# The place of the scaling of energy tile 7 in ScalarE's queue, in a cross-attention kernel on one core

## The chip, the cores and the metric

The kernel runs on one core of a Trainium2 chip. The metric is the time of one execution in microseconds (us) on the device. Engines are named as in the profile: PE is TensorE's matmuls and PEld its weight loads, DVE is VectorE, ACT is ScalarE, POOL is GpSimd, SP issues most of the DMAs.

## The reference

For each of 32 batches there are `x` and `y` of 256 channels by 1024 positions. Cut to what matters:

```
x_q = einsum('oc,bcn->bno', w_qk, y)
x_k = einsum('oc,bcn->bon', w_qk, x)
x_v = einsum('oc,bcn->bon', w_v, x) + b_v
energy = einsum('bnc,bcm->bnm', x_q, x_k)          # 1024 x 1024 for each batch
attention = softmax(energy, axis=-1)
attention = attention / (1e-07 + attention.sum(axis=1, keepdims=True))
x_r = einsum('bcn,bnm->bcm', x_v, attention)
x_r = relu(einsum('oc,bcn->bon', w_t, x - x_r) + b_t)
out = x + x_r
```

The softmax goes along rows of the energy matrix; the second division goes by sums over its columns, so all rows of a batch must be done before the attention is complete.

## The kernel before

**Energies.** Since `w_qk` serves queries and keys alike, the kernel forms g = (w_qk^T w_qk) x once per batch, and a row of energies is y^T g. Both operands are split into parts that TensorE multiplies in one pass: `yf` and `gf` hold, for 2 blocks of 128 channels, three forms each (index 0, 1, 2). A tile of energies (class `Energy`, line 420) is 128 rows by 1024 columns and fills a pair of PSUM banks. `NT` is 8, so a batch has tiles 0 to 7; tile n uses pair n mod 4 of the eight banks (in the last batch, 31, pair n mod 3).

A tile goes through five steps:

- `first()`: 8 matmuls of 128 by 512 (forms 0 and 1, two channel blocks, two halves of the columns; the first half's four come first).
- `scaled()`: ACT multiplies the pair in place by the constant `-OVER`. For tiles 0 to 6 this is one instruction over 1024 columns. For tile 7 it is two, of 512 columns, one for each bank.
- `second()`: 4 matmuls (form 2), added on top of the scaled values, two for each half. Then a DVE reduce over the 1024 columns takes the minimum into `nm`, a column of 128 numbers.
- `exp()`: ACT reads the pair and writes `e`, row block n, with `nm` as bias, and a second ACT instruction reads out the row sums `rs`.
- `share()`: DVE takes the reciprocal `ri` of `rs` and adds `e * ri` to `acc`, the column sums of the batch.

**The order.** The wrappers `pe`, `dve`, `act`, `pool` (class `InOrder`, line 62) keep each engine's instructions in the order in which the program writes them. So the code is the schedule: an instruction that waits holds back all that is written behind it for the same engine. Engines wait for one another by semaphores that follow from the tiles' reads and writes.

The loop over n (line 712) writes the work of a batch as `first(n)`, `exp(n-2)`, `scaled(n)`, `second(n-1)`, `share(n-2)`. On PE this gives `first(7)`, `second(6)`, and behind the loop `second(7)`. On ACT it gives `exp(4)`, `scaled(6)`, `exp(5)`, `scaled(7)` (two instructions), and behind the loop `exp(6)`, two copies out of PSUM, `exp(7)`. On DVE it gives the reduce of tile 5, `share(4)`, the reduce of tile 6, and behind the loop the reduce of tile 7, `share(5)`, `share(6)`, `share(7)`.

**Behind the loop** (line 740 on), for all batches but the last: seven products of half size for the next batch's g (class `Keys`; its products `p1` to `p7` use banks 0, 1 and 2, and `kept` copies a bank to SBUF on ACT: `p1s`, `p5s`, `w`), interleaved with seven for the next batch's values (class `Values`, banks 3, 4 and 5). DVE meanwhile does the three shares, sums `acc` into column totals (`columns`, `inverse`) and gets their reciprocals `rc`. Then `Attention.run` (line 557): DVE's `normal` multiplies `e` by `ri` and `rc` in pieces of 128 by 512, and `mix` forms sums of its quadrants in `et` (`t1`, `t2`, `t3`, `t4`); PE's `epart` multiplies `e` and `et` into three PSUM banks. The quadrant sum `t1` comes in two pieces (`mix(self.t1, ..., j)`, j = 0 and 1), and the product `epart(self.two, 5)`, 8 matmul instructions, reads the first piece with its first four and the second with its last four. The eviction and the stores follow, and the next batch's energies.

Of the kernel before, what the change touches and what calls it, by code (L numbers as in the profile page):

```python
# [17 lines left out]
def kernel(  # L18
# [26 lines left out]
    NT = N // P  # L45
# [41 lines left out]
    def load(b, pieces=1):  # L87
        to = xp.tile([P, KC, N], F32, tag="x", name=f"x_{b}")
        from_ = x[b].rearrange("(k p) n -> p k n", p=P)
        W = KC // pieces  # L90
        for j in range(pieces):
            nc.sync.dma_start(to[:, ts(j, W)], from_[:, ts(j, W)])
        loaded[b] = to
# [115 lines left out]
    def temp(tag, name):  # L209
        return cp.tile([P, MB], F32, tag=tag, name=name)  # L210
# [8 lines left out]
    def summed(b):  # L219

        s = up.tile([P, 4, MB], F32, tag="xs", name=f"xs_{b}")
        t1, t3, t4, t2 = (s[:, j] for j in range(4))
        to = loaded[b]
        b11, b12 = to[:, 0, ts(0, MB)], to[:, 0, ts(1, MB)]
        b21, b22 = to[:, 1, ts(0, MB)], to[:, 1, ts(1, MB)]
        if b == 0:
            pool.tensor_tensor(t1, b11, b12, ALU.add)
            pool.tensor_tensor(t2, b22, t1, ALU.add)
            pool.tensor_tensor(t3, b12, b22, ALU.add)
            pool.tensor_tensor(t4, b21, t2, ALU.add)  # L230
            steps = []
        else:
            q = quarters(x[b])
            nc.sync.dma_start(s[:, :2], q[:, 0, 1:2, :].to_broadcast([P, 2, MB]))
            nc.sync.dma_start(s[:, 2:], q[:, 1])
            steps = [
                lambda: accumulate(s[:, :2], corners(x[b])),
                lambda: accumulate(s[:, 2:], s[:, 0:1].to_broadcast([P, 2, MB])),
                lambda: accumulate(t4, q[:, 1, 1]),
            ]  # L240
        return (b11, b21, b22, t4, t1, t2, t3), steps
# [389 lines left out]
    def columns(b):  # L631

        dve.tensor_reduce(
            parts[:, :, 0],
            acc.rearrange("p (j r) -> p j r", r=G32),
            AX.X,
            ALU.add,
            apply_transpose=True,
        )
# [5 lines left out]
    def inverse(b):  # L645


        sc = one.tile([P, NB, 1], F32, tag="sc", name=f"sc_{b}")
        s = sc[:, :, 0]
        for a in range(1, NG):  # L650
            moved(parts[:G32, :, a], parts[ts(a, G32), :, 0])
        dve.tensor_reduce(s[:G32], parts[:G32], AX.X, ALU.add)
        dve.reciprocal(s[:G32], s[:G32])
        moved(s[G32 : 2 * G32], s[:G32])
        moved(s[2 * G32 :], s[: 2 * G32])
        rc = one.tile([P, NB, G32], F32, tag="rc", name=f"rc_{b}")
        dve.transpose(rc.rearrange("p j r -> p (j r)"), sc.to_broadcast([P, NB, G32]))
        return rc.rearrange("p j r -> p (j r)")
# [49 lines left out]
    for b in range(B):  # L708
        more = b + 1 < B
        rows = []  # L710

        for n in range(NT):
            now = Energy(b, n, q.to, g.split.to)
            rows.append(now)
            now.first()
            if n > 1:
                rows[n - 2].exp()
            now.scaled()
            if n == 1:
                e = ep.tile([P, NT, N], F32, tag="e", name=f"e_{b}")  # L720
                acc = one.tile([P, N], F32, tag="acc", name=f"acc_{b}")
            if n > 0:
                rows[n - 1].second()
            if b == 0 and n == 1:
                u.p4()
                u.c21()
                xsteps[1]()
                xsteps[2]()
                ur, usteps = u.factors()
                for step in usteps:  # L730
                    step()
            if more and b > 0 and n == 0:
                load(b + 1)
                xn, xsteps = summed(b + 1)
            if 1 < n < NT - 1:
                rows[n - 2].share()
            if more and b > 0 and n in (2, 4, 6):
                xsteps[n // 2 - 1]()

        if more:  # L740
            q = Queries(b + 1)
            for i in range(KC):
                q.load(i, nc.sync.dma_start)
            g = Keys(b + 1, xn)
            rows[-1].second()
            rows[-2].exp()
            rows[-3].share()
            g.p1()
            g.p5()
            rows[-1].exp()  # L750
            rows[-2].share()
            rows[-1].share()
            g.p2()
            g.p6()
            columns(b)
            g.p3()
            un = Values(b + 1, xn)
            un.p1()
            g.p7()
            g.c11()  # L760
            g.c12()
            un.p5()
            un.p2()
            un.p6()
            g.c22()
        else:
            rows[-1].second()
            rows[-2].exp()
            rows[-3].share()
            before.xpart(before.one, 7, True)  # L770
            rows[-1].exp()
            rows[-2].share()
            before.epart(before.one, 7)
            ur, usteps = u.factors()
            now = Attention(b, xr, ur)
            now.begin()
            rows[-1].share()
            columns(b)
            for step in usteps:
                step()  # L780
            before.p7s = temp("w", "p7s")
            act.copy(before.p7s, before.one)
        rc = inverse(b)
        if more:
            q.parts(0)
            q.lower(0)
            un.p3()
            g.p4()
            g.c21()
            un.p7()  # L790
            q.parts(1)
            q.lower(1)
            q.mixed(0)
            g.split.parts(0)
            q.mixed(1)
            g.split.lower(0)

            def between():
                g.split.parts(1)
                g.split.lower(1)  # L800
                g.split.mixed(0)
                g.split.mixed(1)

            now = Attention(b, xr, ur)
            now.begin()
            now.run(un, between=between)
            pool.tensor_copy(behind, now.t4[:, HT - 1, :1])
            if b + 2 < B:
                now.close()
                ur, usteps = un.factors()  # L810
                for step in usteps:
                    step()
            else:
                now.epart(now.two, 3, (3,))
                now.c12()
                now.put()
            before = now
            xr, u = xn, un
        else:
            before.end()  # L820
            now.run(None, before)
            now.finish()
# [30 lines left out]
```

## Time and profile before

| | |
|---|---|
| time of 3 runs | 2110.22, 2110.35, 2110.40 us (median 2110.35) |
| time of the profiled execution | 2109.47 us |
| its span in the trace | 2107.7 us |
| granted TensorE clock | 1.0 |
| busy | PE 2083.9 us (99%), DVE 1778.4 (84%), ACT 1150.8 (55%), POOL 674.3 (32%) |
| reduce into `nm`, 256 of them | 1.225 us each |
| exponential, 256 of them | 1.12 us each |

A busy PE is not a PE at its peak: the profile models the ends of matmuls, and a wait shorter than such an end does not show as idle time. Nearly all instructions carry line 73, that of the wrapper, so groups are told apart by what they write and read: `banks<-gf,yf` are energies, `nm<-banks` the reduces, `e<-banks,nm` the exponentials, `banks<-banks` on ACT the scalings. An execution repeats the same pattern once per batch, 65.13 us apart.

### The profile page before, as it was taken

How to read it: one execution, taken by the hardware profiler on the slowest of the kernel's cores; microseconds unless marked ns; L12 is line 12 of the kernel's file. 1: busy time of each engine (PE TensorE's matmuls, PEld its weight loads, DVE VectorE, ACT ScalarE, POOL GpSimd, SP SyncE). 2: the span in 40 equal slices, each digit the busy share in tenths (PEclk: the TensorE clock that was granted, in tenths of full speed). 3: DMA queues.
4: the chain of work that ended last, by engine and by line, in shares of the span. 5: the costliest groups of instructions: out<-in, count | busy, mean ns of one | idle time of the engine just before them, and what ended most of it. 6: DMA issues, size and time to landing. Idle time of an engine off the chain costs nothing.

```text
span 2107.7 us, 21688 instructions
## 1 busy us (share of the span) xinstructions
PE 2083.9 (99%) x7586; PEld 1283.9 (61%) x7586; DVE 1778.4 (84%) x2264; ACT 1150.8 (55%) x1570; POOL 674.3 (32%) x574
## 2 busy tenths in 40 slices
PE   8999999999999999999999999999999999999999
PEld 6556656566665666656665556655566665666664
DVE  6898888988888988889888898888988888988898
ACT  5456554565455664556645556554565455664562
POOL 3322333323333133332333322333323333133321
PEclk9999999999999999999999999999999999999999
DMA  4756577665776656766558766577665776656740
GB/s 140 169 121 145 130 175 170 129 148 128 165 174 148 132 133 152 180 156 132 137 136 184 168 123 142 132 176 169 127 146 129 169 170 146 137 130 157 180 95 30
DMA packets 107788, 306.03 MB, mean 145 GB/s; under 512 B 10656, under 2 KB 11424, under 8 KB 107680
## 3 DMA queue, kind: packets, MB, share of 16 engines
q0 software_dynamic: 57040, 170.68, 44.2%
q1 hardware_dynamic: 50496, 133.85, 18.7%
q8 instruction: 60, 0.98, 0.2%
q14 instruction: 48, 0.39, 0.1%
q10 hardware_dynamic: 144, 0.13, 0.0%
HBM read 124.78 MB, written 33.55 MB: 75 GB/s over the span
## 4 chain that ended last, share of the span: by engine, by line
PE 91%; DVE 3%; ACT 3%; issue 0%; DVEq 0%
PE banks L73 91%; DVE nm L73 2%; ACT e L73 2%; ACT banks L73 1%; DVE e L73 1%; DVE et L73 0%; DVE acc L73 0%; DVE parts L73 0%; DVE rc L73 0%; DVE sc L73 0%; DVEq L73 0%; DVE z L73 0%; DVE ri L73 0%
## 5 line engine op out<-in xcount | busy, mean ns | idle before, releaser
L73 PE MATMUL banks<-gf,yf 128*128 128x512 f32 x3072 | 726.2, 395 | 13.5 <-ACT banks L73 13.4
L73 PEld LDWEIGHTS banks<-gf,yf 128*128 128x128 f32 x3072 | 571.2, 188 | 162.3 <-ACT banks L73 33.3
L73 DVE TENSOR_REDUCE nm<-banks 128x1 f32<-128x1024 f32 x256 | 313.5, 1225 | 158.3 <-PE banks L73 145.6
L73 ACT ACTIVATE e<-banks,nm 128x1024 f32<-128x1024 f32 x256 | 286.7, 1120 | 154.2 <-DVE nm L73 154.2
L73 PE MATMUL banks<-et,us 128*128 128x512 f32 x768 | 348.8, 596 | 1.0 <-DVE et L73 1.0
L73 DVE SCALAR_TENSOR_TENSOR e<-e,ri,rc 128x512 f32<-128x512 f32 x512 | 347.7, 746 | 1.1
L73 DVE SCALAR_TENSOR_TENSOR acc<-e,ri,acc 128x1024 f32<-128x1024 f32 x224 | 289.3, 1291 | 8.0
L73 ACT ACTIVATE banks<-banks 128x1024 f32<-128x1024 f32 (+1 forms) x288 | 261.2, 915 | 49.0 <-PE banks L73 48.8
L73 PEld LDWEIGHTS banks<-et,us 128*128 128x128 f32 x768 | 143.2, 190 | 191.1 <-issue 161.7
L73 PE MATMUL banks<-e,ut 128*128 128x512 f32 x512 | 225.0, 592 | 0.0
L73 POOL DMA_DIRECT2D yf<-yfr x62 | 53.1, 856 | 528.9 <-ACT yf L73 528.9
L73 ACT ACTIVATE z<-banks,bt 128x512 f32<-128x512 f32 x31 | 21.4, 689 | 340.0 <-DMA out_dram<-z 340.0
L73 PEld LDWEIGHTS banks<-e,ut 128*128 128x128 f32 x512 | 97.2, 190 | 122.7 <-issue 100.2
L73 DVE TENSOR_TENSOR et<-e 128x1024 f32<-128x1024 f32 x128 | 153.7, 1222 | 4.4
L73 POOL TENSOR_TENSOR ut<-ut,bu 128x1024 f32<-128x1024 f32 x64 | 155.5, 2536 | 0.0
L73 POOL DMA_DIRECT2D gf<-gf x62 | 53.1, 856 | 301.5 <-DMA gf<-gfr 257.5
L73 DVE SCALAR_TENSOR_TENSOR z<-z,x 128x512 f32<-128x512 f32 x96 | 136.2, 1419 | 3.3
L73 ACT ACTIVATE yf<-yf 128x1024 fp32r<-128x1024 f32 x124 | 124.3, 1050 | 2.0
L73 PE MATMUL banks<-e,us 128*128 128x512 f32 x256 | 125.3, 592 | 0.0
L73 ACT ACTIVATE gf<-gf 128x1024 fp32r<-128x1024 f32 x124 | 124.2, 1049 | 2.0
L73 POOL DMA_DIRECT2D xs<-xs x31 | 37.2, 1201 | 261.1 <-DMA xs<-in_x_dram 251.6
L73 PEld LDWEIGHTS banks<-wvtTs,xs 128*128 128x128 f32 x768 | 98.2, 192 | 29.6 <-issue 29.6
(104 smaller groups left out, 2614.3 us busy)
## 6 DMA issues: line engine op xcount, KB each, us to landing
yfr<-in_ctx_dram SPq DMA_DIRECT2D x64, 512.0 KB, 5.7
out_dram<-z SPq DMA_DIRECT2D x128, 256.0 KB, 3.4
x<-in_x_dram SPq DMA_DIRECT2D x31, 1024.0 KB, 7.6
xs<-in_x_dram SPq DMA_DIRECT2D x62, 512.0 KB, 5.0
yf<-yfr POOLq DMA_DIRECT2D x62, 512.0 KB, 5.1
yf<-yf POOLq DMA_DIRECT2D x62, 512.0 KB, 7.9
gf<-gfr POOLq DMA_DIRECT2D x62, 512.0 KB, 10.3
gf<-gf POOLq DMA_DIRECT2D x62, 512.0 KB, 5.2
```

The costliest lines, as they stand in the source:

```text
L73: self.last = getattr(self.engine, name)(*args, **kwargs)
```

## The change

In a batch's last turn of the loop (n = 7) the scaling of tile 7 is written ahead of the exponential of tile 5. All other turns keep the exponential in front, and nothing is added or taken away.

```diff
             now.first()
+            order = [now.scaled]
             if n > 1:
-                rows[n - 2].exp()
-            now.scaled()
+                order.insert(int(n + 1 == NT), rows[n - 2].exp)
+            for step in order:
+                step()
             if n == 1:
```

On ACT the order `scaled(6)`, `exp(5)`, `scaled(7)`, `exp(6)` becomes `scaled(6)`, `scaled(7)`, `exp(5)`, `exp(6)`. The queues of the other engines keep their order.

## The prediction

> **What bounds the kernel now.** I read the page first, then the chain of waits, then the timelines of PE, ACT and DVE around one batch's last energy tile. The page:
>
> ```profile
> PE 2083.9 (99%) x7586; PEld 1283.9 (61%) x7586; DVE 1778.4 (84%) x2264; ACT 1150.8 (55%) x1570; POOL 674.3 (32%) x574
> ...
> PE banks L73 91%; DVE nm L73 2%; ACT e L73 2%; ACT banks L73 1%; DVE e L73 1%; DVE et L73 0%; DVE acc L73 0%; DVE parts L73 0%; DVE rc L73 0%; DVE sc L73 0%; DVEq L73 0%; DVE z L73 0%; DVE ri L73 0%
> ```
>
> PE carries 91% of the chain; a reduce, an exponential and a scaling carry nearly all the rest. The chain in order of time shows where:
>
> ```profile
> 1024.52 1.24 DVE nm L73
> 1025.78 1.21 ACT e L73 x2
> 1026.98 0.50 ACT banks L73
> 1027.48 0.04 issue
> 1027.53 62.03 PE banks L73 x224
> ```
>
> So once per batch the chain leaves PE: reduce of tile 5, exponential 5, scaling of tile 7, and then PE again for 62.03 us. The batches are 65.13 us apart, and the same five pieces stand in each. ACT and DVE there (start, duration, engine, operation; in brackets the idle time before and what ended it):
>
> ```profile
> 1025.78 1.12 ACT L73 ACTIVATE e<-banks,nm 128x1024 f32<-128x1024 f32 x1 [0.60 <-DVE nm L73]
> 1026.79 0.19 ACT L73 ACTIVATION_READ_ACCUMULATOR e<-banks,nm 128x1 f32 x1
> 1026.88 1.07 ACT L73 ACTIVATE banks<-banks 128x512 f32<-128x512 f32 x2
> 1028.50 1.11 ACT L73 ACTIVATE e<-banks,nm 128x1024 f32<-128x1024 f32 x1 [0.54 <-DVE nm L73]
> ...
> 1027.24 1.23 DVE L73 TENSOR_REDUCE nm<-banks 128x1 f32<-128x1024 f32 x1
> 1028.85 1.23 DVE L73 TENSOR_REDUCE nm<-banks 128x1 f32<-128x1024 f32 x1 [0.39 <-PE banks L73]
> 1029.99 0.15 DVE L73 RECIPROCAL ri<-rs 128x1 f32<-128x1 f32 x1
> ```
>
> And PE, with one wait of its weight loads 23 us later:
>
> ```profile
> 1025.84 1.29 PE L73 MATMUL banks<-gf,yf 128*128 128x512 f32 x5
> 1027.53 1.22 PE L73 MATMUL banks<-gf,yf 128*128 128x512 f32 x4 [0.39 <-ACT banks L73]
> 1028.58 1.02 PE L73 MATMUL banks<-x,g 128*128 128x512 f32 x2
> ...
> 1051.10 0.30 PEld L73 LDWEIGHTS banks<-et,us 128*128 128x128 f32 x2 [0.66 <-DVE et L73]
> ```
>
> The five matmuls from 1025.84 are the last of `first(7)` and the four of `second(6)`; the four from 1027.53 are `second(7)`. Matmuls of this shape start 0.227 us apart (12 of them to a tile's 2.72), so `second(7)` could have started at 1025.84 + 5 x 0.227 = 1026.97. It starts 0.56 late, and its four take 1.05 instead of 0.91, since its second half waits for the second scaling. PE loses 0.70 us in this place, of which the page's idle column names 0.39.
>
> **The change, part by part.** No instruction is added or removed; three keep their durations and change places on ACT.
>
> *Scaling 7 moved ahead.* Its first half needs the first four matmuls of `first(7)`: the fourth starts at 1025.84 - 4 x 0.227 = 1024.93, ends 0.39 later at 1025.32. ACT comes free of the scaling of tile 6 at about 1025.2 (1024.16 + 1.01). The second half needs the last one, 1025.84 + 0.39 = 1026.23; with 0.04 for the semaphore it runs from 1026.27 to 1026.83 (0.56). Both are done before PE ends `second(6)` and wants the tile at 1026.97. The whole 0.70 of PE's loss goes, if nothing else comes late.
>
> *Exponential 5 behind it.* It is ready at 1025.75 (end of its reduce) and now waits in the queue for the second half. The two halves stand 0.52 apart, start to start, so it starts at about 1026.27 + 0.52 = 1026.79, 1.0 later than now. Queued behind it on ACT is exponential 6, which starts at 1028.50 because its reduce ends at 1028.46. Exponential to next instruction takes 1.10 (1025.78 to 1026.88), so ACT is free at 1027.89: 0.61 to spare, and the delay ends there. Who waits for exponential 5: `share(5)` on DVE, which comes behind two reduces, at 1029.5 at the earliest; and the product that overwrites its bank, `g.p2`, at 1030.30 now and about 1029.6 then. Its sums are out by 1028.0. So this edit costs nothing; without that cover its price is 1.0 us per batch less the 0.61.
>
> *Reduce of tile 7.* It starts at 1028.85 now because `second(7)` ends late. With the 0.70 back, PE has the tile ready near 1028.15. But DVE started the reduce of tile 6 at 1027.24, and that one does not move: its four matmuls lie ahead of the wait. How soon a reduce follows a reduce without a wait no row shows directly. The nearest row is the reciprocal behind the reduce, 1028.85 to 1029.99, 1.14, found so 189 times. The other side is the batch in which the two reduces came closest, 1.26 apart. I take 1.14, since the queue's next instruction reads other data in both cases. So the reduce starts at 1028.38 instead of 1028.85: DVE gains 1.61 - 1.14 = 0.47, not 0.70.
>
> The Trainium skill ("VectorE: DVE Perf Modes", The DRAIN you can't avoid) says that the next operation does not start until the pipe is empty, though one that is not held may start earlier. Taken strictly that makes the spacing a full 1.225, where the row above shows 1.14; the sum below would then be 12.7 us, an estimate, instead of 15.4.
>
> *Which of the two gains counts.* DVE works without a gap from this reduce through shares, column sums, `normal` and the two pieces of `t1` until 1051.04. PE works from 1027.53 without a wait until it needs the second piece of `t1`: the weight load at 1051.10 is released by it. Eight matmuls there take 3.53 (1049.39 to 1052.92) instead of 8 x 0.43 = 3.43, so 0.10 is already lost. DVE is thus level with PE at 1051, and PE, arriving 0.70 earlier, will wait until DVE is done, 0.47 earlier. The batch gains 0.47; PE's wait for `t1` grows from 0.10 to about 0.33 us. Nothing in DVE's chain may lag: exponential 7 starts at 1030.98 now, behind two copies that follow `g.p1` and `g.p5`. Then the copies start at 1029.60 and 1030.08, exponential 7 at 1030.56, its sums come at 1031.77, and `share(7)` wants them at 1032.78 - 0.47 = 1032.31. That leaves 0.54.
>
> *Behind 1051* both engines are shifted by 0.47, and so are the stores, POOL's adds and DMA issues that hang on them. The next energies start on PE 0.47 earlier. Period: 65.13 to about 64.66.
>
> *The sum.* By the distances of the two reduces: 27 batches have 1.61, so 27 x 0.47 = 12.7. The first has 2.20 (gain 1.06), the last 1.41 (0.27; there too DVE's chain sets the end, as PE waits for `e` and `et`), and three have 1.26, 1.79 and 1.76 (0.12, 0.65, 0.62). Together 2.7, in all 15.4 us. The profiled execution of 2109.47 us (span 2107.7) would become 2094.1. The median of the runs lies 0.88 above the profiled one, and 2110.35 - 15.4 = 2095.0.
>
> Bounds: with the reduces 1.26 apart the gain is 0.12 less in each of 32 batches, 15.4 - 3.8 = 11.6, giving 2098.8. With PE's whole loss back it is 27 x 0.70 = 18.9, and for the five others 1.21, 0.70, 1.05, 0.85 and 0.50 by their own gaps: 23.2, giving 2087.2.
>
> **The rivals.**
>
> *DVE does not hold PE* (8%): the whole 0.70 comes back. For it: PE is 91% of the chain, DVE's waits are far smaller. Against: the weight load at 1051.10 waits for DVE. Time about 2087.
>
> *The second scaling is released later than I think* (9%), so that the change does only part of what it says. Now both halves start behind exponential 5, when every matmul they could wait for is done. So the trace does not show whether the second waits for the last matmul of `first(7)` or for the last of `second(6)`. In the latter case it starts at 1026.74 + 0.39 + 0.04 = 1027.17 instead of 1027.40: 0.23 gain for PE and the reduce alike. 27 x 0.23 = 6.2, and some 2 from the others: 2102.
>
> *Slower* (3%): exponential 5 becomes late for what follows. The place is ACT's queue: exponential 5, then 6, two copies, 7, and `share(7)` on DVE. There is 0.61 to spare at exponential 6 and 0.54 at `share(7)`. The delay beyond the 1.0 counted must pass 1.15 before DVE feels it, and 1.15 + 0.47 = 1.62 before the batch is slower than now. If the scaling were held for one tile's turn more (2.72), a batch would lose 2.72 - 1.62 = 1.10, in all 34 us: about 2144. Against it: `first(7)` is finished on PE before all this and waits for nothing that ACT does later.
>
> *No change* (3%): PE loses at another wait what it gains here, the one for `t1` growing by 0.70. This needs DVE's reduce to stay at 1028.85, with PE's end of `second(7)` no longer its reason. Nothing points to it. Time 2110.
>
> **How the numbers follow.** The forecast holds 77%. The range 2089 to 2102 takes in its upper bound 2098.8 and reaches up to the second rival and most of the way down to the first. Differences below 0.2% (4.2 us) can't be told from no change here. Faster by more than that are the forecast and the first two rivals, 94%; within it 3%; slower 3%.
>
> **What would show it.** In the changed profile ACT should have the two scalings of 512 columns ahead of exponential 5, and the exponential starting about 1.0 after the end of its reduce instead of at once. PE's matmuls of `second(7)` should follow `second(6)` 0.227 apart, and the 13.4 us of PE waiting for ACT's `banks` should be gone. The reduces of tiles 6 and 7 should stand 1.14 apart, exponential 6 should still start right behind its reduce, and the weight load for the second piece of `t1` should wait longer by 0.2 to 0.25. The chain should no longer hold the reduce, exponential and scaling of this place; it should pass through DVE's shares, `normal` and `t1` instead. Wrong would be: reduces further apart than 1.3, a wait in `share(5)` or `share(7)` for `rs`, or a batch period not near 64.66.

## The result and the profile after

The changed kernel takes 2096.4 us (median of 6 runs, 2095.36 to 2097.67) against 2110.38 us of the kernel before (6 runs, 2110.22 to 2110.73). The ratio is 0.9934, 95% interval 0.9921 to 0.9946: a small gain, clear of the noise. The forecast was 2095.0, range 2089 to 2102. The profiled execution took 2096.0 us (span 2094.2), 13.5 less than the profiled one before; the forecast had 15.4.

The page of the changed kernel, busy time and the chain of waits by line:

```profile
PE 2080.7 (99%) x7586; PEld 1289.2 (62%) x7586; DVE 1774.5 (85%) x2264; ACT 1145.9 (55%) x1570; POOL 674.7 (32%) x574
...
PE banks L73 72%; DVE e L73 12%; DVE et L73 4%; DVE gfr L73 3%; DVE rc L73 2%; DVE sc L73 2%; DVE parts L73 1%; DVE acc L73 1%; DVE nm L73 0%; DMA gf<-gf 0%; DVEq L73 0%; DVE ri L73 0%; DVE z L73 0%; ACT ow L73 0%
```

Busy shares tell nothing: PE has 99% as before. The chain does: PE falls from 91% to 72%. The reduce, the exponential and the scaling are out of it, and DVE's work between the column sums and `t1` has come in. The timeline of the same batch as in the prediction, 6.49 us earlier by now:

```profile
1018.93 0.58 ACT L73 ACTIVATE banks<-banks 128x512 f32<-128x512 f32 x1 [0.24 <-PE banks L73]
...
1019.77 0.58 ACT L73 ACTIVATE banks<-banks 128x512 f32<-128x512 f32 x1 [0.27 <-PE banks L73]
1020.27 1.11 ACT L73 ACTIVATE e<-banks,nm 128x1024 f32<-128x1024 f32 x1
1020.75 2.35 DVE L73 TENSOR_REDUCE nm<-banks 128x1 f32<-128x1024 f32 x2
...
1022.01 1.11 ACT L73 ACTIVATE e<-banks,nm 128x1024 f32<-128x1024 f32 x1 [0.54 <-DVE nm L73]
```

The two scalings stand ahead of exponential 5, each started by PE. The exponential starts 1.0 after its reduce has ended (1018.03 + 1.22 = 1019.25), and exponential 6 still starts as soon as its own reduce is done. The two reduces are one line now (x2), without a gap: 1.14 apart instead of 1.61. PE in the same place, one run of twelve matmuls without a break (the last four of `first(7)`, then `second(6)` and `second(7)`) and then the next batch's product:

```profile
1018.67 2.88 PE L73 MATMUL banks<-gf,yf 128*128 128x512 f32 x12
1021.39 1.02 PE L73 MATMUL banks<-x,g 128*128 128x512 f32 x2
```

12 x 0.227 = 2.72 is the whole distance, so the 0.70 us are back. Further on, the weight load for the second piece of `t1`, the eight matmuls that read `t1`, and where the chain passes to them:

```profile
1044.14 0.30 PEld L73 LDWEIGHTS banks<-et,us 128*128 128x128 f32 x2 [0.89 <-DVE et L73]
```

```profile
1042.20 3.93 PE L73 MATMUL banks<-et,us 128*128 128x512 f32 x8
```

```profile
1041.50 1.33 DVE e L73 x2
1042.84 0.02 issue
1042.86 1.24 DVE et L73
1044.10 0.04 issue
```

The weight load waits 0.89 instead of 0.66, and the eight matmuls take 3.93 instead of 3.69. Of PE's time 0.33 us are lost here in each batch, where 0.10 were lost before. The period is 64.67 us (65.13 before).

### The profile page after: what moved, and what is told of

Its sections match the earlier page's. It is cut to its first block, busy times and chain, and to the rows that moved or that the text cites. A ratio compares the mean times of both kernels' runs of the same rounds, so it can differ in the third digit from the quotient of the medians.

```text
span 2094.2 us, 21719 instructions
## 1 busy us (share of the span) xinstructions
PE 2080.7 (99%) x7586; PEld 1289.2 (62%) x7586; DVE 1774.5 (85%) x2264; ACT 1145.9 (55%) x1570; POOL 674.7 (32%) x574
## 4 chain that ended last, share of the span: by engine, by line
PE 72%; DVE 24%; issue 1%; DMA 0%; DVEq 0%; ACT 0%
PE banks L73 72%; DVE e L73 12%; DVE et L73 4%; DVE gfr L73 3%; DVE rc L73 2%; DVE sc L73 2%; DVE parts L73 1%; DVE acc L73 1%; DVE nm L73 0%; DMA gf<-gf 0%; DVEq L73 0%; DVE ri L73 0%; DVE z L73 0%; ACT ow L73 0%
## 5 line engine op out<-in xcount | busy, mean ns | idle before, releaser
L73 PE MATMUL banks<-gf,yf 128*128 128x512 f32 x3072 | 716.3, 394 | 0.3 <-DMA gf<-gf 0.3
L73 PE MATMUL banks<-et,us 128*128 128x512 f32 x768 | 353.9, 597 | 3.1 <-DVE et L73 1.4
```

Of the source, the lines that this page charges most:

```text
L73: self.last = getattr(self.engine, name)(*args, **kwargs)
```

## The experiments

Each was timed against the kernel before in five rounds; kernels shown together ran on one chip and share its runs of before. Periods and distances are medians over the batches of the profiled execution.

### DVE's chain against PE's own gap: four kernels on one chip

The changed kernel again:

> The changed kernel itself, beside the three below on one chip. Both theories: about 2096.4 us, a batch period of 64.67, the reduces of tiles 6 and 7 1.14 apart, PE waiting 0.23 longer at the second piece of t1 than before the change.

Measured: 2094.96 us, ratio 0.9931 (0.9919 to 0.9944); period 64.67, reduces 1.14 apart, 0.33 lost at `t1`. This is the measure for the other three.

Only the first half of the scaling moved:

```diff
-            order = [now.scaled]
-            if n > 1:
-                order.insert(int(n + 1 == NT), rows[n - 2].exp)
-            for step in order:
-                step()
+            if n + 1 == NT:
+                now.scaled((0,))
+                rows[n - 2].exp()
+                now.scaled((1,))
+            else:
+                ...
```

> Only the first half of the scaling of tile 7 goes ahead of exponential 5; the second half stays behind it. Exponential 5 would start at 1025.92 in the batch shown, the second half at 1027.02 and end at 1027.58, so PE waits about 0.3 us for the second half of tile 7 where the changed kernel waits for nothing. Theory (DVE's chain from the reduce of tile 7 to t1 sets the batch, and PE has 0.23 to 0.33 us to spare there): the reduce starts about 1028.46 instead of 1028.38, so a batch loses 0.1 and the time is 2097 to 2101. Rival (what PE loses in this place is what counts): 0.3 x 31 = 9 us, about 2106.

Measured: 2098.25 us, ratio 0.995 (0.9936 to 0.9963), 3.3 us above the changed kernel. Its timeline:

```profile
1021.35 0.60 ACT L73 ACTIVATE banks<-banks 128x512 f32<-128x512 f32 x1
1021.59 2.47 DVE L73 TENSOR_REDUCE nm<-banks 128x1 f32<-128x1024 f32 x2
1022.00 0.30 PEld L73 LDWEIGHTS banks<-gf,yf 128*128 128x128 f32 x2 [0.49 <-ACT banks L73]
```

PE loses 0.34 us in `second(7)` and the reduces are 1.25 apart, 0.11 more than in the changed kernel. A batch is longer by 0.12 (period 64.79), not by 0.34. PE waits less at `t1` in return, 0.10 instead of 0.33. So PE's gap is not what a batch pays; the place of the reduce on DVE is.

DVE relieved in both kernels, the addition of tile 5 to the column sums left out:

```diff
             if self.n == 0:
                 dve.tensor_scalar(acc, row, ri, None, ALU.mult)
-            else:
+            elif self.n != 5:
                 dve.scalar_tensor_tensor(acc, row, ri, acc, ALU.mult, ALU.add)
```

> The kernel before with DVE relieved: the addition of tile 5 to the column sums is left out (1.2 us of DVE per batch, between the reduce of tile 7 and t1). Theory: only the 0.10 us per batch that PE loses at t1 comes back, 3 us, so about 2107. Rival (DVE's chain plays no part): 2110.

> The changed kernel with the same addition of tile 5 left out. Theory: PE's wait of 0.33 us at t1 goes, so that the whole 0.70 of the first wait and the 0.10 of t1 come back; batch period 65.13 - 0.70 - 0.10 = 64.33 and 10 us less than the changed kernel, about 2086. Rival (the 0.23 us that did not come back went elsewhere, to stores or POOL): no faster than the changed kernel, 2096.

Measured: 2105.64 us without the change, ratio 0.9981 (0.9972 to 0.999), and 2082.5 with it, ratio 0.9874 (0.986 to 0.9887). The wait at `t1` is zero in both; with the change, the eight matmuls that read `t1` now run at their full pace:

```profile
1036.62 3.60 PE L73 MATMUL banks<-et,us 128*128 128x512 f32 x8
```

Between these two the change is worth 23.1 us. With DVE's full work it is worth 14.5 (2109.5 to 2094.96). The periods are 65.06 and 64.33, a difference of 0.73 per batch, where PE's gap is 0.70. The missing 0.23 us of each batch are therefore PE's longer wait for DVE at `t1`.

Both times are below what was expected, 1.4 us under 2107 and 3.5 us under 2086. The period of 64.33 is the expected one; of the 12.5 us to the changed kernel 2.7 lie behind tile 6 of the last batch but one, and the expectation had counted repeating batches alone.

One sum covers all kernels of this section to 0.03: the period is 64.33 plus what PE loses in `second(7)` and at `t1`. That is 0.70 + 0.10 before the change (65.13), 0 + 0.33 after it (64.67), 0.34 + 0.10 with half of the scaling moved (64.79), and 0.70 + 0 in the old order with DVE relieved (65.06).

### Taking the wait at `t1` away without leaving anything out

```diff
             self.epart(self.three, 2)
+            self.xpart(self.one, 6, True)
             self.epart(self.two, 5)
             self.p5s = self.biased(self.two, "p5s", bt[:, 1, :])
-            self.xpart(self.one, 6, True)
```

> The changed kernel with one product of the attention moved in PE's order: xpart(self.one, 6), 0.86 us that need nothing of DVE's, goes ahead of epart(self.two, 5), the product that reads t1. Nothing is left out. Theory (PE only waits there because it arrives 0.33 us before the second piece of t1): PE comes 0.86 later to t1, the wait of 0.33 goes, the eviction of self.two comes about 0.5 later and may cost up to 0.1; a batch gains 0.25 to 0.33, the period is 64.34 to 64.42 and the time 2085 to 2088. Rival (DVE's chain sets the batch also behind t1): period 64.67, about 2095.

Measured: 2089.6 us, ratio 0.9907 (0.9893 to 0.992), period 64.49. The wait at `t1` is gone, but of the 0.33 only 0.18 stay gained. What comes late next, on ACT and on PE's weight loads of this kernel:

```profile
1044.03 0.69 ACT L73 ACTIVATE op5s<-banks,bt 128x512 f32<-128x512 f32 x1 [2.81 <-PE banks L73]
...
1044.77 0.30 PEld L73 LDWEIGHTS banks<-x,wtTs 128*128 128x128 f32 x2
```

The eviction of `self.two` ends at 1044.72, and `xpart(self.two, 3)`, which writes that bank, begins right behind it. PE loses 0.15 per batch there, more than the 0.1 allowed for: 0.33 less 0.15 is the 0.18 by which the period falls, and leaves it 0.07 above the expected 64.34 to 64.42. No other kernel here that does the whole work is faster.

### How late exponential 5 may come

Small multiplications were put on ACT between the scaling and exponential 5 of the changed kernel, one and six:

```diff
                 order.insert(int(n + 1 == NT), rows[n - 2].exp)
+            if n + 1 == NT:
+                for _ in range(6):
+                    order.insert(1, lambda: act.mul(few, few, 1.0))
```

> The changed kernel with one small extra multiplication on ACT (128 columns in place, about 0.3 us) between the scaling of tile 7 and exponential 5. Theory (exponential 5 may come 0.6 us later still before exponential 6 moves): no change against the changed kernel, 2095. Rival (every delay of exponential 5 costs the batch): 0.3 x 31 = 9 us, 2104.

> The same with six such multiplications, one behind the other, about 1.9 us in all. This passes the spare time. Theory: exponential 6 moves by 1.9 - 0.6 = 1.3; the copy p1s behind it, which PE's product p6 waits for without spare time, moves as much; of PE's 1.3 the 0.33 that it waits at t1 are covered. DVE waits for the sums of tile 7, 0.5 of 1.3 covered, so 0.8. A batch loses 0.8 to 1.0, 25 to 31 us: 2120 to 2126, slower than the kernel before. Rival (ACT is not on the path, 55% busy): 2095 to 2100.

Measured: one costs nothing (2096.03 us, ratio 0.9936, 0.992 to 0.995, period 64.67). Six cost the whole gain and more: 2120.09 us, ratio 1.005 (1.0037 to 1.0063), period 65.49. ACT with six, and the two largest named waits of PE's weight loads over that execution:

```profile
1030.23 2.01 ACT L73 ACTIVATE few<-few 128x128 f32<-128x128 f32 x6
1032.15 1.10 ACT L73 ACTIVATE e<-banks,nm 128x1024 f32<-128x1024 f32 x1
...
1033.24 1.10 ACT L73 ACTIVATE e<-banks,nm 128x1024 f32<-128x1024 f32 x1
...
1034.33 0.58 ACT L73 COPY gp1s<-banks 128x512 f32<-128x512 f32 x1
```

```profile
PEld banks L73 <- ACT gp1s L73: 39.4, 31, 1.3
PEld banks L73 <- ACT e L73: 31.8, 36, 1.0
```

Exponential 6 no longer waits for its reduce; it follows exponential 5. PE then waits twice: `g.p2` for the bank that exponential 5 reads, and `g.p6` for the copy behind exponential 6. In the batch shown PE loses 1.15 us by them, and no longer the 0.33 at `t1`; the difference is the 0.82 by which the period grew, and it lies in the expected 0.8 to 1.0. So a delay of exponential 5 does cost time once it passes the time to spare, as the prediction's slower rival had it. The path is another one: the rival went by DVE's `share(7)`, and DVE does wait for row sums (0.30 at `share(5)`, 0.29 at `share(7)`), but PE's own waits are longer and set the batch.

### The scaling ahead in every turn

```diff
-                order.insert(int(n + 1 == NT), rows[n - 2].exp)
+                order.append(rows[n - 2].exp)
```

> The scaling goes ahead of the exponential in every turn of the loop, not in the last alone. Theory: in the other turns PE stands in no wait for the scaling (its matmuls start 0.227 apart throughout), so nothing is to be gained; the exponentials come about 1.5 later, of which 1.4 are covered before DVE's share needs their sums. Time as the changed kernel within 3 us, 2093 to 2098. Rival (a scaling further ahead always helps): 0.2 or more per turn, below 2080.

Measured: 2100.57 us, ratio 0.9958 (0.9945 to 0.997), above the expected 2093 to 2098. The period is 64.59, 0.08 below the changed kernel's (PE loses 0.26 at `t1` instead of 0.33): nothing much to gain in the other turns, as expected. The loss lies in the last batch, where the stretch from its predecessor's tile 6 to the end is 6.35 us longer (109.58 against 103.23). PE waits five times there for an exponential, 6.7 us in all, twice as follows:

```profile
2037.39 3.04 PE L73 MATMUL banks<-gf,yf 128*128 128x512 f32 x12 [1.36 <-ACT e L73]
2041.78 3.04 PE L73 MATMUL banks<-gf,yf 128*128 128x512 f32 x12 [1.35 <-ACT e L73]
```

The last batch has three pairs of banks, so `first(n)` needs the exponential of tile n - 3, and a delay of the exponential stands on PE's path at once. The expectation had looked at the four-pair batches alone.

### The last batch

In the changed kernel's last batch one addition of DVE's shares takes 2.34 us; all others there take 1.28. POOL's first addition is beside it (DVE, then POOL):

```profile
2051.88 1.28 DVE L73 SCALAR_TENSOR_TENSOR acc<-e,ri,acc 128x1024 f32<-128x1024 f32 x1
...
2053.27 2.34 DVE L73 SCALAR_TENSOR_TENSOR acc<-e,ri,acc 128x1024 f32<-128x1024 f32 x1
```

```profile
2053.26 1.27 POOL L73 TENSOR_TENSOR us<-ut 128x512 f32<-128x512 f32 x1 [20.94 <-PE banks L73]
```

Before the change POOL's addition began 0.21 us behind DVE's, and it was POOL's that took longer (2.20), which nobody waits for. To test it, the last batch got its old order back:

```diff
-                order.insert(int(n + 1 == NT), rows[n - 2].exp)
+                order.insert(int(n + 1 == NT and more), rows[n - 2].exp)
```

> The changed kernel, but the last batch keeps the order of the kernel before (exponential 5 ahead of the scaling). Theory (in the last batch the change lets POOL's first addition start 0.01 us ahead of share(7) on DVE, which then takes 2.34 us instead of 1.28; with the old order POOL starts 0.2 behind it): share(7) of the last batch takes 1.28 again, and the stretch from its start to the end of the span is 40.2 us instead of 40.95. The batch loses its 0.27 at the reduce, so about 0.5 us less than the changed kernel, 2095, which the time alone can hardly show. Rival (the long share(7) is chance): it is long again, or short in the changed kernel too.

> Both edits on the changed kernel: xpart(self.one, 6) ahead of epart(self.two, 5), and the old order in the last batch. Theory: period 64.49 as with the first edit alone, share(7) of the last batch 1.28, 0.5 us less than with the first edit alone: 2089. Rival (the edits disturb each other): 2092 or more.

Measured: 2094.78 us, ratio 0.9929 (0.9915 to 0.9942), and with both edits 2090.41, ratio 0.9907 (0.9894 to 0.9921). The times can't show 0.5 us, and both edits together are no better in time than the first alone (2089 was expected; the period is 64.49 as expected). The traces do show it. With the old order:

```profile
2052.16 1.28 DVE L73 SCALAR_TENSOR_TENSOR acc<-e,ri,acc 128x1024 f32<-128x1024 f32 x1
```

```profile
2052.37 2.19 POOL L73 TENSOR_TENSOR us<-ut 128x512 f32<-128x512 f32 x1 [21.02 <-PE banks L73]
```

POOL is behind again, and the stretch from the start of `share(7)` to the end of the span is 40.23 us (40.22 with both edits) against 40.96 in the changed kernel. In five kernels of this study POOL's addition began ahead and DVE's took 2.10 to 2.34 us; in the other seven, where POOL's came behind, it took 1.28.

## Why the prediction was right, step by step

**The scaling moved ahead.** Right to a hundredth: the second half was put at 1026.27, which is 1019.78 in the changed kernel's time, and it started at 1019.77, released by the last matmul of `first(7)`. The rival of a later release falls with this line. PE's 0.70 went completely.

**Exponential 5.** Late by 1.0 and without cost, as said. One extra multiplication (0.3 us) left the time as it was and six (1.9) made it slower than before, so the time to spare ends between the two; the 0.61 itself was not tested. ACT's idle time ahead of exponential 6 in the changed kernel, 0.54, fits it. The list of those who wait was short by one: `g.p6`, whose weight load in the changed kernel starts as soon as the copy `p1s` behind exponential 6 is done, with nothing to spare. The margin of 1.62 before a batch is slower than in the kernel before left it out. For 1.9 it would give 0.3, and the period with six is 0.36 above the old one; as this came by PE's waits and not by `share(7)`, the agreement is luck.

**The reduce of tile 7.** The nearest row, 1.14, was the right choice: the distance is 1.14 in all batches but the first. A spacing of a whole 1.225, the strict reading of the Trainium skill ("VectorE: DVE Perf Modes", The DRAIN you can't avoid), is not what this case measures.

**Which gain counts.** DVE's 0.47, not PE's 0.70. Period 64.67 against the forecast 64.66, wait at `t1` 0.33 as forecast. The four kernels on one chip show the cause: relieve DVE, and the rest of the 0.70 appears. The rival that DVE doesn't hold PE is refuted by the same runs. The chain names one link that the timeline does not bear out: it leaves DVE for PE at the first `gfr`. DVE starts that instruction 1.17 behind the one before it, in the kernel before as in the changed one, so it did not wait for PE.

**The sum.** Between tile 6 of the second batch and tile 6 of the last but one the forecast was 27 x 0.47 + 0.12 + 0.65 = 13.46, the profile has 13.30 (1889.30 to 1876.00). The two ends were mis-sized, both in the same direction:

- The first batch was put at 1.06; tile 6 of the second batch is only 0.37 earlier. Its two reduces stand 1.33 apart, not 1.14, so the change brought 0.86 there (its period falls from 65.75 to 64.89). The rest is that its own tile 6 comes 0.48 later (49.63 to 50.11). At 18 to 20 us, long before the changed lines, TensorE's granted clock was half in this execution, here before and then after:

```profile
18.00:20.00 2.00, 2.00 (x11) 1.77 (x10) 0.00 (x0) 2.00 (x3) 1.05 (x1) 1.00 0.68 180
```

```profile
18.00:20.00 2.00, 2.00 (x5) 1.33 (x4) 0.00 (x0) 1.37 (x2) 0.87 (x1) 0.50 0.71 188
```

  (the third number from the end is the granted clock). The first energies start 1.18 us later. The program up to there is the same in both kernels. The clock there was 1.00 in two of the experiments, one with the old order and one with the new, and half for some microseconds in the others; in the three kernels with 1.00 the first energies start at 25.87 to 26.77 us, in the nine with the half clock at 27.00 to 29.23. So this is a difference of executions. The Trainium skill ("TensorE: Matmul & The Clock Gate", Part 1) says that the clock is halved until the array has been busy for a window of about 3.4 us, and that the window runs free of the kernel's start, which fits this trace: by its rows from 16 to 22 us (0.70, 0.50, 0.94) the clock was half for about 3.4 us. Why it fell there is not shown.
- The last two batches were put at 0.62 + 0.27; they lost 0.2 instead, 1.1 less than the forecast. The step at fault for 0.7 of it is "POOL's adds ... that hang on them" being shifted along: in the last batch POOL's addition is released by PE and came ahead of DVE's `share(7)`, which then took 1.05 longer and made the stretch to the end 0.73 longer. The other 0.4 lie at the start of the last batch, where PE in the changed kernel waits for the DMA that brings `gf` for it:

```profile
2025.29 4.47 PE L73 MATMUL banks<-gf,yf 128*128 128x512 f32 x17
2030.04 6.35 PE L73 MATMUL banks<-gf,yf 128*128 128x512 f32 x26 [0.29 <-DMA gf<-gf]
```

  The kernel before has no such break. Neither has the changed kernel with the old order in the last batch, which is the same program up to there: from tile 7 of the last batch but one to tile 0 of the last it takes 38.50 us, against 38.94 here and 38.53 before the change. So the new order alone does not bring this wait; what makes the DMA late is not shown.

The 0.7 of the first batch, the 1.1 of the last two and 0.16 between them are the 1.9 us by which the profiled gain fell short.

## What to carry to other kernels

When a wait is removed from the busiest engine, follow each other engine that was waiting beside it, and work out how far its own queue lets it move up: where the two are already level at the place where they meet next, the batch gains the smaller of the two amounts, and the rest turns up as a longer wait there. In an in-order queue, an instruction that stalls the busiest engine may go ahead of one whose readers come later, as far as the time to spare reaches; count that time at every reader, in the odd first and last iterations too. The wait that is left at the meeting point can be filled with work that does not depend on the late engine.

## What the runs showed of the hardware

Of a DVE addition of two SBUF tiles and a POOL addition that start almost together, the one that starts later takes about 1 us more: DVE's 2.34 instead of 1.28 where it started 0.01 us behind, POOL's 2.20 instead of 1.27 where it started 0.21 behind. The Trainium skill ("SBUF — State Buffer", Who interferes with whom) says that a VectorE instruction with two inputs in SBUF contends with a GpSimd instruction that reads SBUF, and that issue order decides who blocks, which agrees with these rows. Here a shift of 0.2 us between two engines turned a delay that cost nothing into one on the path.
